# A four layer graph network on one core: side steps beside the differences get a half tile of their own

## The chip, the core and the metric

The kernel runs on one core of a Trainium2 chip. The core has five engines with instruction queues of their own: TensorE (PE in the profile; PEld is its loading of weights), VectorE (DVE), ScalarE (ACT), GpSimd (POOL) and SyncE (SP), which here issues the DMAs. Each engine takes its instructions in order, and one that waits holds up all behind it on that engine. The metric is the time of one execution on the device in microseconds; lower is better.

## The reference

There are 128 graphs of 128 nodes with 64 features, and a 128 x 128 adjacency matrix each, about an eighth of whose entries are not zero. Four layers follow each other. Each normalizes x over the features, clips it at zero, and adds what a small graph network makes of the result:

```python
# layer 0, h = relu(layernorm(x)); mask = adj > 0
xj_proj = x @ W1a
diff = x[:, :, None, :] - x[:, None, :, :]
h = jax.nn.relu(xj_proj[:, :, None, :] + diff @ W1b + b1)
hm = jnp.einsum('bjkh,bjk->bjh', h, mask)
return hm @ W2 + deg[..., None] * b2
# layer 1: three times relu(adj @ (h @ W + b)), then (h @ Wout + bout) * nodemask
# layer 2: y = (adj @ x + x) @ W + bias, normalized by its length, batch norm over all nodes, relu
# layer 3: tanh([h, adj @ h] @ W1 + b1) @ W2 + b2
```

Layer 0 needs a clipped sum for every edge, with 192 hidden features (x in these formulas is the layer's h). Layer 2's batch norm needs the mean over all graphs, so layers 2's end and 3 can only follow when every graph has been through layer 2's first part.

## The kernel before

Graphs are taken four at a time: 32 groups. For a group, layer 0 is done as 20 tiles (`ORDER`). The term that belongs to a node j (`psort`) is copied to PSUM, then a product of a selector with one bit per row (`oh`, made by comparing rank numbers on VectorE) and the node features `q` adds the term of that node's i-th neighbour, and VectorE clips the sum at zero and adds it to `acc`. One tile does this for one neighbour rank i of all nodes of the four graphs. To be exact in bf16, `q` is split in three parts. Twelve of the 20 tiles are "near": the first four ranks, with the three parts laid out over partitions by way of DRAM (`q_dram`, `near_q`, `n_dram`, `near_n`), so that each tile needs four products; the other eight are "far" and need twelve, or are made for the fullest rows alone (`psort_r`, `num_r`).

`differences(t)` issues one tile: products of the first two graphs, a fill of the tile after the next (L560), the selector of the tile three ahead (L541 for near ones, L546 for others), a `yield`, products of the last two, and the accumulation (L579 for a group's first tile, L581 on ScalarE for the first of the fullest rows, L583 else) and a second `yield`. So a tile has two halves, and a group 40. Three pairs of PSUM banks hold tiles (`blk`); two banks are left for all else.

Two other lines of work go beside the differences of a group g, as generators that are run a step at a time, up to their next `yield`:

- `prepare(g + 1)`: loads, the transposed adjacency (`adjT`, by TensorE and L391), the mask `mT`, the ranks of the neighbours and the order of the nodes (`rank`, `lower`, `to`), layer 0's norm, `q` and its split (L465 to L468), its way through DRAM (L469, L471), `num` and its way through DRAM (L483, L485), `fro` and `psort` with their copies (L498, L521).
- `after_layer0(g - 1)`: `layer0_end` (the sums `sA` and `sB` put back in node order, times W2), `layer1`, and `layer2_norm`. It takes nearly two groups of time, so two of these run beside each other, half a length apart.

When to take the next step is decided while the program is issued. Each generator has a count of halves since its start, a number of steps (`N_PREPARE` 14, `N_AFTER` 26) and a length in groups (0.8 and 1.9), and the generator that is furthest behind its share is stepped next. It is stepped at once when 2.5 steps late (`LAG`), else only while an estimate of TensorE's time (`spend`, called by every `matmul` and `transpose`) is below a budget that grows by `PACE` a half. A `yield 2` counts two steps. So a step has no place of its own: it depends on both counts and on the products issued until then, and several steps may fall in one half.

The order in which a program issues instructions is not wholly that in which they stand on the engines: in the trace, instructions that were ready stand ahead of others that were issued before them. Issue order decides between what is ready.

After the last group, the rest of the last two `after_layer0` run without differences beside them; then come the batch norm and layer 3.

## Time and profile before

| | |
|---|---|
| median of 3 runs | 1395.79 us (1392.44 to 1399.84) |
| the profiled execution | 1398.05 us |
| its span, first to last instruction | 1396.2 us |
| instructions | 29319 |
| busy: TensorE, VectorE, ScalarE, GpSimd | 1232.2, 1167.8, 990.8, 270.6 us |
| mean granted TensorE clock | 0.979 |
| first accumulation of a group (L579): first, last | 51.75, 1201.77 us |

The span has a start of some 50 us (weights, group 0's preparation), the 32 groups, a stretch to about 1270 us with the last graphs' layers 1 and 2, and the batch norm with layer 3. In a row of the groups view stand the line, the engine, what is written from what, the count, the busy time and the mean of one; in a row of waits: who waited, for whom, the total in us, how often, and the longest. A row of the timeline has the start in us, the duration, the engine and what it did, and in brackets the idle time before it. A row of the windows view has a stretch, its length, and the busy time of each engine with its count of instructions in brackets, then the granted clock, the share of DMA and its rate.

### The profile page before, as it was taken

The page shows a single profiled execution, that of the slowest core. Times are in us where ns is not written, and L with a number is a line of the kernel's source. Part 1 is how long each engine was busy: PE and PEld are TensorE (multiplying, and loading weights), DVE is VectorE, ACT ScalarE, POOL GpSimd, SP SyncE. Part 2 cuts the span into 40 slices and gives each one's busy share as a digit, 9 for nine tenths or more (in the row PEclk, how much of TensorE's full clock was granted, in tenths as well). Part 3 has the DMA queues.
Part 4 walks back from the last instruction along what each step waited for, and adds up shares of the span by engine and source line. Part 5 has one row for each costly group of instructions (what it writes and reads, how often), then busy time and mean ns, then how long its engine had stood idle before and what let it go on. Part 6 is the DMA issues. An engine that isn't in the chain of part 4 may idle for free.

```text
span 1396.2 us, 29319 instructions
## 1 busy us (share of the span) xinstructions
PE 1232.2 (88%) x10964; PEld 959.3 (69%) x10964; DVE 1167.8 (84%) x2629; ACT 990.8 (71%) x1883; POOL 270.6 (19%) x322
## 2 busy tenths in 40 slices
PE   3788999999999999999999999999999999995787
PEld 1467777777777777777777777776777777763566
DVE  6898888888888888888888888888898888866973
ACT  1677777777777777777777777777777777753783
POOL 3111111111111111111111111111111111015830
PEclk9899999999999999999999999999999999997889
DMA  5443222322323222222222222223222212200345
GB/s 120 131 120 98 67 66 78 83 83 84 83 76 83 84 75 75 76 63 75 66 78 84 83 84 83 75 83 84 76 75 79 62 59 60 76 9 15 93 112 126
DMA packets 108788, 110.97 MB, mean 79 GB/s; under 512 B 42895, under 2 KB 88220, under 8 KB 108636
## 3 DMA queue, kind: packets, MB, share of 16 engines
q1 hardware_dynamic: 108636, 109.00, 28.5%
q8 instruction: 89, 1.46, 0.5%
q14 instruction: 63, 0.52, 0.1%
HBM read 52.70 MB, written 35.29 MB: 63 GB/s over the span
## 4 chain that ended last, share of the span: by engine, by line
PE 65%; ACT 17%; DVE 13%; issue 2%; SPq 1%; DMA 1%; DVEq 0%; POOL 0%; ACTq 0%; POOLq 0%
PE blk L103 24%; PE ps_pr L103 10%; ACT blk L560 9%; DVE acc L583 6%; PE ps_ag L103 5%; PE ps_p L103 5%; PE ps_sA L103 5%; PE ps_o L103 3%; PE ps_sB L103 3%; PE ps_q L103 2%; PE ps_ah L103 2%; PE ps_hm L103 2%; ACT q L465 2%; DVE leftT L424 1%; PE ps_key L103 1%
## 5 line engine op out<-in xcount | busy, mean ns | idle before, releaser
L583 DVE SCALAR_TENSOR_TENSOR acc<-blk,acc 128x768 f32<-128x768 f32 x576 | 543.1, 950 | 65.0 <-PE blk L103 38.9
L560 ACT COPY blk<-psort 128x768 f32<-128x768 f32 x544 | 436.1, 806 | 134.1 <-DVE acc L583 132.2
L103 PE MATMUL blk<-q,oh 128*128 128x192 bf16 x3072 | 318.2, 246 | 34.5 <-ACT blk L560 34.3
L103 PEld LDWEIGHTS <-oh 128*128 128x128 bf16 x3072 | 259.1, 98 | 89.3 <-issue 84.3
L103 PE MATMUL blk<-near_q,ohn 128*128 128x192 bf16 x1536 | 199.7, 246 | 22.4 <-ACT blk L560 22.1
L103 PEld LDWEIGHTS <-ohn 128*128 128x128 bf16 x1536 | 134.7, 98 | 59.9 <-issue 45.3
L468 POOL TENSOR_TENSOR q<-rest,q 128x768 bf16<-128x768 f32 x32 | 52.8, 1648 | 209.1 <-ACT q L467 209.1
L642 POOL TENSOR_TENSOR adjT<-adjT,ident 128x512 f32<-128x512 f32 x32 | 41.9, 1310 | 254.8 <-PE ps_ag L103 254.8
L668 POOL TENSOR_TENSOR y<-y,nrm 128x256 f32<-128x256 f32 x32 | 19.7, 615 | 363.7 <-PE blk L103 238.1
L634 ACT COPY msg<-ps_pr 128x512 f32<-128x512 f32 x64 | 37.5, 586 | 68.9 <-PE ps_pr L103 67.5
L541 DVE TENSOR_SCALAR ohn<-near_n 128x1536 bf16<-128x1536 bf16 x128 | 84.3, 695 | 0.0
L103 PE MATMUL ps_pr<-g,dT 128*128 128x128 f32 x512 | 78.8, 288 | 0.8 <-ACT dT L626 0.8
L560 ACT COPY blk<-psort_r 128x768 f32<-128x768 f32 x96 | 77.5, 807 | 0.5 <-DVE acc L583 0.4
L103 PEld LDWEIGHTS ps_pr<-g,dT 128*128 128x128 f32 x512 | 64.3, 191 | 11.5 <-issue 7.2
L103 PE MATMUL ps_ag<-adjT,msg 128*128 128x128 f32 x512 | 71.5, 283 | 0.6 <-ACT msg L634 0.5
L103 PEld LDWEIGHTS <-ones_b 3*128 3x128 bf16 (+2 forms) x280 | 26.0, 93 | 59.1 <-issue 51.5
L103 PEld LDWEIGHTS ps_ag<-adjT,msg 128*128 128x128 f32 x512 | 62.1, 191 | 5.9 <-ACT msg L634 5.5
L103 PE MATMUL ps_p<-wp,hs 128*128 128x384 f32 x128 | 59.0, 543 | 0.0
L626 ACT ACTIVATE dT<-ps_ag 128x512 f32<-128x512 f32 x96 | 56.8, 592 | 3.0 <-PE ps_ag L103 2.8
L103 PE MATMUL ps_q<-wq,hT 128*128 128x384 f32 x128 | 52.5, 534 | 4.4 <-ACT hT L328 0.8
L103 PE MATMUL ps_hm<-ident,h 128*64 128x128 f32 x248 | 43.6, 308 | 14.0 <-ACT h L841 13.9
L103 PE MATMUL ps_sA<-fro,acc 128*128 128x128 f32 x256 | 53.3, 290 | 2.1 <-ACT dT L626 1.9
(220 smaller groups left out, 2544.8 us busy)
## 6 DMA issues: line engine op xcount, KB each, us to landing
q_dram<-q SPq DMA_DIRECT2D x32, 567.0 KB
near_q<-q_dram SPq DMA_DIRECT2D x96, 189.0 KB
near_n<-n_dram SPq DMA_DIRECT2D x96, 126.0 KB
a<-in_adj_dram SPq DMA_DIRECT2D x32, 256.0 KB
adjT_dram<-adjT SPq DMA_DIRECT2D x32, 256.0 KB
adjT<-adjT_dram SPq DMA_DIRECT2D x32, 256.0 KB
psort_r<-psort SPq DMA_DIRECT2D x32, 228.0 KB
fro_r<-fro SPq DMA_DIRECT2D x32, 152.0 KB
```

The costliest lines, as they stand in the source:

```text
L103: return nc.tensor.matmul(o, w, x, **kw)
L424: nc.vector.scalar_tensor_tensor(flat(leftT), pk, float(NEAR), flat(mT), ALU.is_gt, ALU.mult)
L465: nc.scalar.copy(parts_q[:, 0, p, :], pq[:, 0:W])
L468: nc.gpsimd.tensor_tensor(parts_q[:, 2], rest, parts_q[:, 1], ALU.subtract)
L541: nc.vector.tensor_scalar(oh.rearrange("p t b n -> p (t b n)"), near_n[g % 2].rearrange("p t b n -> p (t b n)"), float(i + 1), None, ALU.i ...
L560: nc.scalar.copy(columns(t), psorts[g][in_segments(n)])
L583: nc.vector.scalar_tensor_tensor(acc, o, 0.0, acc, ALU.max, ALU.add)
L626: nc.scalar.activation(flat(dT), pa, AF.Relu)
L634: nc.scalar.copy(flat(msg), pm)
L642: nc.gpsimd.tensor_tensor(adjT, adjT, ident.unsqueeze(1).to_broadcast([P, G, P]), ALU.add)
L668: nc.gpsimd.tensor_tensor(y, y, over_f(nrm), ALU.mult)
```

## The change

Each step now says itself how many halves pass until the next: `yield 3` means three. A generator holds the half at which its next step is due and the half it has reached. At each half, both generators take the steps that are due, whatever the others did. The numbers in the yields come from a search that evens the summed load of the three engines over a group's 40 halves. `prepare` then ends at its half 32, and `after_layer0` at its half 79, so that it takes two whole groups. The estimate of TensorE's time, the budget and their constants go.

Some work moves between steps as well: in `center` the square (L301) is issued with the mean and the centred x instead of a step later; `sA` and `sB` are no longer in adjacent steps, and `sB`'s bank is asked for at its own step; `prepare` takes the rest of its norm at fixed places, and issues `num` with its DMAs in the step that issues the split of `q`, ahead of `hs`, `db` and x's sum on GpSimd.

```diff
-    def matmul(o, w, x, **kw):
-        spend(w, math.prod(x.shape[1:]), x.dtype)
-        return nc.tensor.matmul(o, w, x, **kw)
...
+    matmul, transpose = nc.tensor.matmul, nc.tensor.transpose
...
         nc.vector.scalar_tensor_tensor(xc, over_f(mean), -1.0 / F, xt, ALU.mult, ALU.add)
-        yield
         sq = (once if tag else work).tile([P, G, F], F32, tag="sq" + tag, name="sq")
         nc.scalar.activation(sq, xc, AF.Square)
-        yield
+        yield 3
...
+    def finish(gen):
+
+        while True:
+            try:
+                next(gen)
+            except StopIteration as end:
+                return end.value
...
         mT = once.tile([P, G, P], BF16, tag="mT", name="mT")
-        yield
-        nc.vector.tensor_scalar(mT, adjT, 0.0, None, ALU.is_gt)
         ln = layernorm_relu(xt, "0")
         next(ln)
-        yield
+        yield 4
+        next(ln)
+        nc.vector.tensor_scalar(mT, adjT, 0.0, None, ALU.is_gt)
+        yield 2
         pr = bank("ps_rank")
...
-        yield
+        yield 4
         pr = bank("ps_rank")
...
-        next(ln)
         lower = once.tile([P, G, P], BF16, tag="lower", name="lower")
...
-        yield
+        yield 5
+        h = finish(ln)
+        yield 1
         pl = bank("ps_place")
...
-        next(ln)
-        yield 2
-        h = yield from ln
+        yield 1
         hT = transposed(h, "0")
-        yield
+        yield 3
         rest = once.tile([P, NP, W], F32, tag="rest", name="rest")
         for p in range(NP):
             pq = bank("ps_q")
             matmul(pq[:, 0:W], hT[:, p, :], flat(wq), start=True, stop=True)
-            yield
             nc.scalar.copy(parts_q[:, 0, p, :], pq[:, 0:W])
             nc.vector.tensor_tensor(rest[:, p, :], pq[:, 0:W], parts_q[:, 0, p, :], ALU.subtract)
+            yield 1 + p
         nc.scalar.copy(parts_q[:, 1], rest)
...
-        hs = gathered(h, to, "hs")
-
-        db = once.tile([P, G, F], F32, tag="db", name="db")
-        nc.gpsimd.tensor_tensor(db, over_f(degs[:, :, 0]), over_g(b2_all), ALU.mult)
-        nc.gpsimd.tensor_tensor(xt, xt, db, ALU.add)
-        yield
         pn = bank("ps_num")
...
-        yield
+        yield 2
+        hs = gathered(h, to, "hs")
+
+        db = once.tile([P, G, F], F32, tag="db", name="db")
+        nc.gpsimd.tensor_tensor(db, over_f(degs[:, :, 0]), over_g(b2_all), ALU.mult)
+        nc.gpsimd.tensor_tensor(xt, xt, db, ALU.add)
+        yield 1
         half, at = divmod(g, NG // 2)
...
-        yield
+        yield 3
         psort = edge.tile([P, NP, W], F32, tag="psort", name="psort")
...
             nc.scalar.copy(psort[:, p, :], pp[:, 0:W])
-            yield
+            if p == 0:
+                yield 3
...
     def layer0_end(g):
         xt, (_, _, fro, fro_r) = xs[g], sorts[g]
-
-        pA, pB = bank("ps_sA"), bank("ps_sB")
+        yield 4
+
+        pA = bank("ps_sA")
...
-            if b % 2:
-                yield
+            if b == 1:
+                yield 1
         nc.scalar.copy(flat(sA), pA)
+        yield 10
+        pB = bank("ps_sB")
...
         nc.scalar.copy(flat(sB), pB[:, 0 : NP * P])
-        yield 2
+        yield 9
...
-        for nxt, nrow, width in ((g1, "L1_gnn_b1", P), (g2, "L1_gnn_b2", P), (gout, "L1_gnn_bout", F)):
+        for nxt, nrow, width, wait in ((g1, "L1_gnn_b1", P, 3), (g2, "L1_gnn_b2", P, 3), (gout, "L1_gnn_bout", F, 4)):
...
-            yield
+            yield wait
...
-            yield
+            yield 7 if nxt is g1 else 3
...
-                    budget += PACE
-                    for s in side:
-                        s[3] += 1
-                    while side:
-                        late, s = max(((s[2] * s[3] / (nyields * s[4]) - s[1], s) for s in side), key=lambda k: k[0])
-                        if late <= 0 or (spent["us"] >= budget and late < LAG):
-                            break
-                        step = next(s[0], "end")
-                        s[1] += 1 if step is None else step if step != "end" else 0
-                        if step == "end":
-                            side.remove(s)
-                    budget = min(budget, spent["us"] + PACE)
+                    for s in list(side):
+                        while s in side and s[1] <= s[2]:
+                            step = next(s[0], None)
+                            if step is None:
+                                side.remove(s)
+                            else:
+                                s[1] += step
+                        s[2] += 1
```

In the norm (`layernorm_relu`) the two later steps follow after 3 and 3 halves, and `h` after 2; the other yields behind layer 0 become 3 (its end), 3 (`ah`), 4 (layer 1's end), 3 (`zT`), 3 (`py`), 2 (`nrm`) and 1 (`counted`).

## The prediction

> **What bounds the kernel now.** I read the page's busy times and slices first, to see whether one engine bounds the span.
>
> ```profile
> PE 1232.2 (88%) x10964; PEld 959.3 (69%) x10964; DVE 1167.8 (84%) x2629; ACT 990.8 (71%) x1883; POOL 270.6 (19%) x322
> PE   3788999999999999999999999999999999995787
> DVE  6898888888888888888888888888898888866973
> ACT  1677777777777777777777777777777777753783
> ```
>
> The kernel is one long steady stretch (slices 4 to 34) in which TensorE and VectorE are both nearly full and neither is full. Ends of products are modelled, so TensorE's nines overstate it. The steady stretch repeats by group, and a group starts with the one line L579. Its starts 600.00, 637.89, 675.68, 712.76 give 112.76/3 = 37.6 us a group. Next, the busy time of each engine in one group, cut where tiles 0, 5, 10 and 15 are accumulated:
>
> ```profile
> core 0: us, PE busy (x) PEld busy (x) DVE busy (x) ACT busy (x) POOL busy (x), PEclk, DMA share, GB/s
> 600.00:609.55 9.55, 8.95 (x95) 7.56 (x95) 8.48 (x17) 5.96 (x10) 2.61 (x3) 1.00 0.19 60
> 609.55:619.67 10.12, 8.30 (x75) 6.66 (x75) 9.06 (x21) 6.62 (x13) 1.34 (x2) 1.00 0.00 0
> 619.67:626.43 6.76, 6.32 (x59) 4.60 (x56) 6.73 (x19) 6.34 (x13) 1.65 (x1) 1.00 0.42 133
> 626.43:637.89 11.46, 11.45 (x90) 8.49 (x89) 8.52 (x20) 9.59 (x20) 0.61 (x1) 1.00 0.57 127
> ```
>
> Five tiles take 6.76 us in one place and 11.46 in another. VectorE is the fuller in the second and third rows (9.06 of 10.12, 6.73 of 6.76), TensorE in the first and last (11.45 of 11.46). That is what uneven placement looks like: each engine has its own crowded part and is short of work elsewhere. The waits say the same, over 32 groups:
>
> ```profile
> ACT blk L560 <- DVE acc L583: 132.6, 153, 2.4
> PE blk L103 <- ACT blk L560: 60.1, 107, 1.6
> DVE acc L583 <- PE blk L103: 38.9, 65, 1.6
> DVE mT L413 <- ACT adjT L391: 33.2, 29, 1.9
> PEld ps_sB L103 <- DVE leftT L424: 23.8, 29, 0.8
> ```
>
> The first three are the loop of the differences itself (fill, product, accumulate), each engine waiting for another in turn. The last two are side steps issued too close to what they need. Last, the end of a group, from the timeline:
>
> ```profile
> 619.70 1.65 POOL L468 TENSOR_TENSOR q<-rest,q 128x768 bf16<-128x768 f32 x1 [6.45 <-ACT q L467]
> 621.38 0.34 SPq L469 DMA_DIRECT2D q_dram<-q  x1
> 627.94 1.23 SPq L485 DMA_DIRECT2D near_n<-n_dram  x3
> 634.26 0.60 PE L108 MATMUL ps_aT<-ident,a 128*128 128x128 f32 x4
> 635.28 1.02 DVE L541 TENSOR_SCALAR ohn<-near_n 128x1536 bf16<-128x1536 bf16 x2
> 637.36 0.49 PE L103 MATMUL blk<-near_q,ohn 128*128 128x192 bf16 x4
> 637.89 0.96 DVE L579 SCALAR_TENSOR_TENSOR acc<-blk,extra 128x768 f32<-128x768 f32 x1 [0.89 <-PE blk L103]
> ```
>
> Here the reader sees a second chain: the split of q goes through POOL, SP and DRAM, and only its return lets the next group's tile 0 be made. The next group's transposes (634.26) already stand ahead of that tile on TensorE, although they are issued after it. So issue order is a preference: what is ready can be put ahead.
>
> **The change, part by part.** No instruction is added or dropped, so the engines' busy sums stay. The removed TensorE estimate issued nothing. What changes is where in the 40 half tiles of a group each side step is issued. I price a step by starts apart in the timeline where the engine does not idle (an accumulation 0.87 though its row says 0.95, a fill 0.73, a far half tile's six passes 0.50, a near one's two 0.17, an f32 pass 0.11). The positions before come from following the two counters and the budget through one group; those after are the sums of the yields.
>
> ```
> step (TensorE, VectorE, ScalarE us)   half before -> after
> prepare: transpose .44/0/.47          0 -> 0
>   first norm part 0/.66/.32           4, 10 -> 0
>   its var 0/.33/.20; h 0/.43/0        14; 14 -> 4; 15
>   mT 0/.34/0                          4 -> 4
>   rank1 .44/1.27/0                    8 -> 6
>   rank2 .65/2.10/0                    10 -> 10
>   place .11/.60/0; hT .22/0/.27       14; 16 -> 16; 17
>   q products .66/.46/.37 twice        17, 18, 20 -> 20, 21
>   last q cast 0/0/.81; num .22/0/.57  20; 22 -> 23; 23
>   hs .44/0/.27; fro .32/.58/.48       20; 25 -> 25; 26
>   psort .91/0/.37 twice; extra 0/0/1.38   27, 30; 32 -> 29, 32; 32
> after layer 0: sA .90 twice; copy .48 0, 4; 8 -> 4, 5; 5
>   sB .87/0/.33; po 1.34/.33/0         8; 14 -> 15; 24
>   ah, first ag and dT                 29; 32 -> 35; 38
>   (second group) pm, ag, pm, ag, gout 35, 38, 1, 5, 11 -> 1, 8, 11, 14, 18
>   zT, py, nrm, counted, sums          24, 27, 31, 34, 36 -> 30, 33, 36, 38, 39
>   two norms: xc, sq, var, h           14, 16, 18, 20 -> 27, 27, 30, 33
>                                       17, 18, 20, 23 -> 22, 22, 25, 28
> ```
>
> Example, VectorE in halves 8 to 11. Before: two accumulations 1.74, rank1 1.27, rank2 2.10, the product with the mask L640 0.34, one selector 0.20: 5.65 us. After: rank1 and L640 are elsewhere, 4.04. Doing this for each four halves, and taking the fullest engine of each:
>
> ```
> halves  0-3  4-7  8-11 12-15 16-19 20-23 24-27 28-31 32-35 36-39  sum
> before 3.83 3.41 5.65  4.55  3.39  3.69  3.82  2.47  3.82  2.67  37.3
> after  2.93 4.34 4.04  3.10  2.88  3.91  3.44  2.69  4.23  2.63  34.2
> ```
>
> The sum before, 37.3, is close to the measured 37.6, so I take this grain. It gives 3.1 us a group as the upper bound of the gain.
>
> Waits that go: sB (half 15) no longer shares its half with rank1 and rank2, whose banks it waited for in 29 groups (23.8 us); mT gets four halves after the transpose instead of a bad place in VectorE's queue (33.2 us). What is late next is ScalarE in halves 20 to 27 and 32 to 35 (3.91 and 4.23 us are its loads), where fills stand behind casts and extra. These terms are inside the table and not added.
>
> One rule of the Trainium skill speaks against this. Perfetto Trace Analysis, in Optimization Strategy, says that the same gap repeating can mean too few buffers for the next tile; the side steps have two banks, and the wait for leftT repeats in 29 groups. By that rule order alone would leave this wait, and the forecast would be 24 us later; the new positions put the bank users in different halves, so I follow the row.
>
> The lower bound comes from the q chain. The last q cast moves from half 20 to 23, and num from 22 to 23, while the halves get shorter. After the cast come POOL's L468, then on SP q_dram, n_dram, three near_q and three near_n; behind those wait fro_r and psort_r, which have the rest of the group. Waiting for near_n on VectorE is L541; behind it would stand the accumulation of tile 0, mT and the next norm. From tile 0 to the cast the table after gives 21.2 (halves 0 to 23) less 2.0 for the first two: 19.2 us; before it was 618.80 - 600.00 = 18.8. From the cast to q_dram 621.38 - 618.80 = 2.6. From q_dram to the next L579 the trace has 14.5 at the shortest (96.92 to 111.38) and 16.5 in the group shown (621.38 to 637.89). So a group bound by this chain takes 19.2 + 2.6 + 14.5 = 36.3, a gain of 1.3, or with 16.5 takes 38.3, a loss of 0.7.
>
> I take 35.3 us, a gain of 2.3: halfway between the evened load with the 0.3 by which the table missed (34.5) and the chain at its shortest (36.3), since the transposes at 634.26 show that a late tile 0 lets the next preparation run ahead and so shortens the chain. Group 1 has half of the old layer work, 1.2; groups 2 to 30 have 29 times 2.3 = 66.7; group 0 (25.50 us, preparation alone, VectorE 24.41 busy) and group 31 and the tail after 1231 keep their time: the same number of steps of the last two groups remains, about 13, and it costs 1 us either way if not.
>
> Moved past other queues at no cost: POOL's adjT L642 (1.3 us) now ends near half 20, before L468; hs needs POOL's cast of to, nine halves earlier; adjT's last reader zT is at half 30 instead of 24, ten halves before its buffer of four is written again. If one of these covers went, its cost would be its own length, at most 1.6 us a group.
>
> Sum against the profiled execution: 1398.05 (span 1396.2 and 1.85 around it) less 67.9 is 1330.1. That execution was 2.3 above the median 1395.79, so 1328.
>
> **The rivals.** First, full evening: group 34.5, 3.1 times 29.5 = 91 us, 1304. For it: 34.5 still leaves VectorE at 32.8 busy. Against: the three engines wait for each other in turn already.
>
> Second, the other side: the q chain becomes the bound. Place: L541 at the group's end. It decides when last cast to next L579 exceeds 37.6 - 19.2 = 18.4 us; the group shown has 19.1. At 38.3 a group it costs 0.7 times 29, 20 us: 1416; if halves stay 0.94 us, 23 of them less one and 19.1 make 39.8 and 1460. For it: L541 stands after tile 19's accumulation now. Against: VectorE's idle time before L541 is nil, so near_n lands earlier than it is used.
>
> Third, the order does little, since ready work is put ahead anyway: 1396. For it: group 0 took 25.50 where the same table gives 30.1. Against: the full groups do agree with the table.
>
> **How the numbers follow.** Likeliest case (35.3) 0.42, full evening 0.22, chain bound 0.26, little change 0.10. A change of 0.5% is about what the runs of this kernel can tell. Faster: 0.42 + 0.22 + 0.04 of the third = 0.68; same 0.06; slower 0.26. The range goes from 1288 (full evening and half a microsecond a group more) to 1412, just short of the chain's first price; alone, the likeliest case has 1310 to 1358 (gains of 2.9 to 1.3).
>
> **What would show it.** Right: L579 about 35.3 us apart; five tiles taking between 8 and 9.5 us everywhere; sB's wait for leftT and mT's for adjT gone; fills waiting for accumulations under 132.6. Wrong: VectorE idle before L541 or before L579 growing past the 0.89 shown, near_n issued within 3 us of the next L579, or ScalarE full in the third quarter with TensorE waiting for fills beyond 60.1.

## The result: 0.55% slower, and the profile after

The changed kernel takes 1406.09 us (median, 1397.23 to 1408.77), the kernel before beside it on the same chip 1398.46. The ratio is 1.0055, with a 95% interval of 1.0044 to 1.0066. The forecast was 1328 us.

The busy times and slices of the changed kernel:

```profile
PE 1230.3 (88%) x10964; PEld 964.5 (69%) x10964; DVE 1150.2 (82%) x2629; ACT 995.6 (71%) x1883; POOL 278.6 (20%) x322
PE   3788999899989989999999999998999999895787
DVE  6798788889889889888878888988988888866873
```

The same work is done, and VectorE's share is lower than before (82%, it was 84%). Its busy time is 17.6 us less, and 17.3 of that lie in the near selectors, first before, then after (busy time, mean ns of one; idle time ahead of them):

```profile
L541 DVE TENSOR_SCALAR ohn<-near_n 128x1536 bf16<-128x1536 bf16 x128 | 84.3, 695 | 0.0
L529 DVE TENSOR_SCALAR ohn<-near_n 128x1536 bf16<-128x1536 bf16 x128 | 67.0, 559 | 0.0
```

The median of one is the same (553 and 552 ns). But before, one selector in each of 28 groups took 1.15 us (the one at 620.62, for instance, beside GpSimd's q, 619.70 to 621.35), and after, none takes over 0.97; that GpSimd's work is the cause was not tried. The forecast did not count on this, and the time does not show it: VectorE waits longer instead.

By the starts of groups (now L567), the profiled execution's span, 8.3 us longer than before, divides into 5.4 up to the start of group 3 (153.54, was 148.13), 0.9 for the 28 groups from there to group 31, and 2.0 behind that. So the groups, of which 2.3 us each had been forecast, gained nothing: they take 0.03 us more each.

Three groups in a row, in the windows view (length, then busy time and number of instructions by engine, the granted clock, DMA):

```profile
core 0: us, PE busy (x) PEld busy (x) DVE busy (x) ACT busy (x) POOL busy (x), PEclk, DMA share, GB/s
563.76:603.10 39.34, 36.01 (x330) 29.10 (x330) 32.88 (x73) 29.08 (x55) 6.56 (x7) 1.00 0.28 78
603.10:641.67 38.57, 34.74 (x316) 27.67 (x315) 32.70 (x71) 28.17 (x53) 6.41 (x7) 1.00 0.28 76
641.67:676.15 34.48, 31.96 (x288) 24.76 (x287) 31.41 (x68) 27.82 (x52) 6.39 (x7) 1.00 0.28 79
```

Groups now come in a cycle of three lengths, 34.5 to 39.3 us (before: 37.1 to 37.9). The last row looks like full evening come true (34.5 was the first rival's group), but its instruction counts say otherwise: 288 products instead of 330. Side work of that group was done in the next one. The mean of the three, 37.5, is what counts.

The waits of the whole span (who waited, for whom, total in us, times, longest):

```profile
ACT blk L548 <- DVE acc L571: 51.2, 113, 1.0
DVE to_b L441 <- PE ps_place L439: 44.7, 30, 1.9
...
PE blk L556 <- ACT blk L548: 37.8, 68, 2.2
DVE acc L571 <- PE blk L556: 36.2, 68, 2.2
...
DVE mT L404 <- ACT adjT L379: 14.8, 20, 1.2
```

Fills waiting for accumulations fell from 132.6 to 51.2 (those that wait for a group's first accumulation rose from 1.7 to 23.7), TensorE's waits for fills from 60.1 to 37.8, mT's from 33.2 to 14.8, and sB's wait for leftT is no longer among them (layer 1's aggregation has some of it now, 8.8 us in 11 groups). But a wait stands on VectorE that the kernel before does not have: `to_b`, the comparison with the sort positions, waits 1.5 us in 30 of 32 groups. The timeline of the second group above shows why:

```profile
613.46 1.16 PE L629 MATMUL ps_ag<-adjT,msg 128*128 128x128 f32 x8 [0.73 <-ACT msg L625]
613.67 0.96 DVE L571 SCALAR_TENSOR_TENSOR acc<-blk,acc 128x768 f32<-128x768 f32 x1
...
614.54 0.45 PE L592 MATMUL ps_sB<-fro,acc 128*64 128x128 f32 x4
...
615.25 0.44 PE L592 MATMUL ps_sB<-fro_r,acc 128*64 128x128 f32 x4
...
615.62 0.67 PE L556 MATMUL blk<-q,oh 128*128 128x192 bf16 x6
...
616.12 0.24 PE L439 MATMUL ps_place<-ones_b,lower 128*128 128x1 bf16 x4
...
616.23 0.66 PE L556 MATMUL blk<-q,oh 128*128 128x192 bf16 x6
616.41 0.69 DVE L441 TENSOR_TENSOR to_b<-row_b,ps_place 128x512 bf16<-128x512 bf16 x1 [1.78 <-PE ps_place L439]
...
617.01 0.95 DVE L571 SCALAR_TENSOR_TENSOR acc<-blk,acc 128x768 f32<-128x768 f32 x1
```

Read TensorE's rows alone: aggregation, then the eight products of sB (half 15 of the table), six products of a tile, and only then the four tiny ones that give the positions (half 16). VectorE is free from 614.63, but the next thing in its queue is `to_b`, and no accumulation can pass it. From 613.67 to 617.01 one accumulation is started in 3.34 us. Neither engine is overloaded in these halves by the prediction's table; one stands behind the other's queue. It does so twice: the accumulation at 617.01 also needs its tile's second six products (616.23, to 616.89), and they too stand behind sB. So these rows don't tell whether the late positions or the late products are the price of sB's place.

### The profile page after: what moved, and what is told of

Its sections match the earlier page's. It is cut to its first block, busy times and chain, and to the rows that moved or that the text cites. A ratio compares the mean times of both kernels' runs of the same rounds, so it can differ in the third digit from the quotient of the medians.

```text
span 1404.5 us, 29255 instructions
## 1 busy us (share of the span) xinstructions
PE 1230.3 (88%) x10964; PEld 964.5 (69%) x10964; DVE 1150.2 (82%) x2629; ACT 995.6 (71%) x1883; POOL 278.6 (20%) x322
## 4 chain that ended last, share of the span: by engine, by line
PE 63%; ACT 16%; DVE 15%; issue 3%; SPq 1%; DMA 1%; POOL 0%; ACTq 0%; DVEq 0%; POOLq 0%
PE blk L556 19%; PE ps_pr L621 7%; DVE acc L571 7%; ACT blk L548 5%; PE ps_ag L629 5%; PE ps_sA L584 3%; PE ps_ga L326 3%; PE ps_p L503 3%; PE ps_sB L592 2%; PE ps_pr L334 2%; PE blk L664 2%; PE ps_hm L829 2%; DVE rest L452 2%; PE ps_o L600 2%; PE ps_o L598 2%
## 5 line engine op out<-in xcount | busy, mean ns | idle before, releaser
L571 DVE SCALAR_TENSOR_TENSOR acc<-blk,acc 128x768 f32<-128x768 f32 x576 | 546.0, 951 | 41.0 <-PE blk L556 36.2
L548 ACT COPY blk<-psort 128x768 f32<-128x768 f32 x544 | 434.6, 807 | 67.4 <-DVE acc L571 38.5
L556 PE MATMUL blk<-q,oh 128*128 128x192 bf16 x3072 | 323.2, 247 | 35.4 <-ACT blk L548 35.2
L617 ACT ACTIVATE dT<-ps_ag 128x512 f32<-128x512 f32 x96 | 57.1, 595 | 41.7 <-PE ps_ag L629 40.6
L471 POOL TENSOR_TENSOR db<-degs,b_all 128x256 f32<-128x256 bf16 x32 | 19.6, 613 | 253.3 <-DVE degs L417 253.3
L529 DVE TENSOR_SCALAR ohn<-near_n 128x1536 bf16<-128x1536 bf16 x128 | 67.0, 559 | 0.0
L441 DVE TENSOR_TENSOR to_b<-row_b,ps_place 128x512 bf16<-128x512 bf16 x32 | 22.0, 686 | 44.7 <-PE ps_place L439 44.7
L450 PE MATMUL ps_q<-wq,hT 128*128 128x384 f32 x128 | 56.1, 525 | 0.8 <-ACT hT L316 0.8
```

Of the source, the lines that this page charges most:

```text
L450: matmul(pq[:, 0:W], hT[:, p, :], flat(wq), start=True, stop=True)
L529: nc.vector.tensor_scalar(oh.rearrange("p t b n -> p (t b n)"), near_n[g % 2].rearrange("p t b n -> p (t b n)"), float(i + 1), None, ALU.i ...
L548: nc.scalar.copy(columns(t), psorts[g][in_segments(n)])
L556: matmul(of(o, b), oh[:, b, :], of(q, b), start=False, stop=True, skip_group_check=True)
L571: nc.vector.scalar_tensor_tensor(acc, o, 0.0, acc, ALU.max, ALU.add)
L617: nc.scalar.activation(flat(dT), pa, AF.Relu)
```

## The experiments

Times are medians, ratios are to the kernel before on the same chip (1397 to 1399 us in all batches), with 95% intervals. "Steady stretch" is 150 to 1180 us of the span, where nothing else is said. "Table" is the sum of the fullest engine over four halves by the prediction's prices (37.3 before, 34.2 after); for the other kernels it was worked out in the same way, and the working isn't shown.

### First: the near tiles, the places, the shared banks

**Two far tiles first in each five.** This gives q, which only near tiles wait for, more time, in the changed kernel and in the kernel before.

```diff
-ORDER = [(NEARS, OTHERS)[k] for k in (0, 1, 0, 1, 0)] * 4
+ORDER = [(NEARS, OTHERS)[k] for k in (1, 1, 0, 0, 0)] * 4
```

> The changed kernel with the order of the 20 tiles of a group turned so that two far tiles come first (pattern far, far, near, near, near instead of near, far, near, far, near); nothing else. A far tile needs nothing that has been through DRAM, so the return of q and num may come two tiles later. Theory of the q chain (the group's end waits for near_n's way through DRAM): the gap between the last accumulation of a group and the first of the next, now 4.8, 6.3 and 3.5 us in three kinds of group, falls to some 2 us in all of them, a group goes from 37.5 to about 35 us, the whole from 1406 to about 1330. Theory of the shared banks (side sums that lie in the banks of the tile buffers tie steps to tiles, so that groups differ by the buffer that tile 0 takes): three kinds of group remain, 1395 to 1406. If the loop of fills, products and accumulations is itself the limit: no change within 10 us.

Measured: 1376.29 us, 0.9862 (0.9824 to 0.9900), faster than both kernels.

> The same turn of the order of tiles in the kernel before. Theory of the q chain: the gap at a group's end there, 4.0 to 4.6 us, falls to some 2 us, a group from 37.6 to 35.5, the whole from 1398 to about 1335; the two kernels then differ by what their placement is worth, the changed one some 10 us or more ahead. Theory of the shared banks: no change in the kernel before, whose groups hardly differ (37.1 to 37.9).

Measured: 1420.84 us, 1.0184 (1.0124 to 1.0244), slower. So it is not that near tiles come too early in general. In the changed kernel VectorE's wait for the positions fell with the order of the tiles, from 40.6 to 4.4 us in the steady stretch; that was the first hint at it.

**Only the preparation put back to the halves it had before.**

```
yield behind     mT rank1 rank2  h  to  hT  num  hs  fro
changed kernel    2   4     5    1   1   3   2    1   3
this run          4   2     4    0   2   1   0    5   2
```

> The changed kernel with fixed places, but the steps of the preparation put where the kernel before has them: rank1 at half 8, rank2 10, the rest of the norm and place 14, hT 16, q products 17 and 18, last cast, num and hs 20, fro 25, psort 27 and 30; the older group's steps stay at their new places. Theory of the q chain: the cast three halves earlier brings tile 0 of the next group forward by up to 2.8 us, so groups of 35 to 36 us and about 1350. Theory of the shared banks: three kinds of group, 1400 to 1410. If the evening of loads is what counts, it gets slower, as VectorE's crowd at half 14 is back: 1410 to 1440.

Measured: 1392.94 us, 0.9966 (0.9954 to 0.9978). The wait for the positions is 27.7 us there.

**The two sums that share a tile's banks given banks of their own.** `degs`' product and `ysum` lie in the banks of the differences' tiles, which go round in three; the edit takes them to the two side banks.

```diff
-        pd = degs_at[:, half, at * 2 * G : (at + 1) * 2 * G]
+        pd = bank("ps_pd")[:, 0 : 2 * G]
...
-        add_sums(ysum, counted, y)
+        pb = bank("ps_ys")
+        for p in range(NP):
+            matmul(pb[0:G, p * P : (p + 1) * P], counted, y[:, 2 * p : 2 * p + 2, :].rearrange("p b f -> p (b f)"), start=True, stop=True)
+        nc.vector.tensor_tensor(flat(ysum), flat(ysum), pb[0:G, 0 : NP * P], ALU.add)
```

> The changed kernel with the two side sums taken out of the banks of the tile buffers: the sorted degrees go to a side bank of their own, and the sums for the batch norm's mean to a side bank per group, added up in SBUF by one more small VectorE instruction a group (about 0.2 us). Theory of the shared banks: the groups of 39.3 and 38.6 us become like the one of 34.5, so all near 35 us and the whole near 1320. Theory of the q chain: the gaps at the end of a group stay at 3.5 to 6.3 us, and the whole moves by less than 15 us.

Measured: 1437.22 us, 1.0281 (1.0256 to 1.0307). The cycle of three lengths is gone (38.2 us a group, 39.7 where the clock fell), so the shared banks have to do with the cycle. Banks of their own do not make the kernel faster; but the edit also asks twice more for the two side banks and adds a VectorE instruction a group, so it does not price the sharing by itself.

### Second: the way through DRAM, and the places one by one

**q and num read in SBUF.** The near tiles read `q` and `num` where they are made; the DMAs are issued as before, and nobody reads what they bring. The near tiles' values are then not the reference's. The same two lines in both kernels:

```diff
-  nc.vector.tensor_scalar(oh.rearrange("p t b n -> p (t b n)"), near_n[g % 2].rearrange("p t b n -> p (t b n)"), float(i + 1), None, ALU.is_equal)
+  nc.vector.tensor_scalar(oh, sorts[g][0].unsqueeze(1).to_broadcast([P, 3, G, P]), float(i + 1), None, ALU.is_equal)
...
-  q = (proj if third is None else near_q)[g % 2][:, part]
+  q = proj[g % 2][:, part]
```

> The changed kernel with the near tiles made from what lies in SBUF already: the selectors compare num itself (shown three times by a broadcast), and the products read a part of q in place of near_q. All DMAs through DRAM are still issued and land, but nothing reads them; products, fills, accumulations and their sizes are the same, the values of the near tiles are not the reference's. Theory of the q chain: this is the whole price of the way through DRAM; tile 0 of the next group needs only num (half 23) and stands where it was issued, the gap at a group's end falls from 3.5 to 6.3 to about 2 us, and the whole goes from 1406 to about 1330. If the end of a group is only where lateness shows that has its cause elsewhere: 1370 to 1400, with the gap turning up in other tiles, as with the far tiles first (1376).

Measured: 1402.01 us, 1.0037 (1.0020 to 1.0055).

> The same in the kernel before. Theory of the q chain: also some 50 us or more faster than 1398, and the distance between this and the changed kernel without the way through DRAM is what the new places are worth by themselves (2.3 us a group, 67 us, by the forecast). If the way through DRAM costs nothing here: 1390 to 1400.

Measured: 1390.68 us, 0.9944 (0.9926 to 0.9962). The edit is not free: reading `num` by a broadcast, a near selector takes 944 ns (median) in the changed kernel and 943 in the one before, where it took 552 and 553, and VectorE's busy time grows by 45.4 and 20.9 us. So the gains of 0.2 and 0.6% are what is left after that, and do not price the return from DRAM. In the changed kernel the gain lies in the start: the first accumulation comes at 44.84 instead of 55.84 us, while a group from group 3 to group 31 takes 37.6 us, as it did. That the chain does not bound the groups there is read from the trace of the changed kernel: in the group from 603.10 the last near_n is issued by 631.18 us, the selectors that read it start at 640.27, and VectorE has no wait ahead of them in any group.

**The older group's steps put back to the halves they had, alone and with the preparation's.** These are the halves at which the counters and the budget of before had taken them.

```
yield            start  sA  sA copied  sB  po  h  msg1  msg2  dT3  x  zT  py  nrm  counted
changed kernel     4     1     10       9   3  2    7     3    4   4   3   3   2     1
this run           0     4      4       6   0  9    3     4    6   6   2   4   3     2
```

(`h` here is layer 1's norm; `msg1`, `msg2` and `dT3` are the messages and the last clipped product of layer 1; `x` is its end.)

> The changed kernel with only the older group's steps at the places of the kernel before, the preparation at its new ones. With the preparation at its old places the changed kernel took 1392.9. If the evening of the older group's steps is what gains and the later preparation what loses: slower than 1406, about 1415 to 1440. If neither matters: 1395 to 1410.

Measured: 1431.56 us, 1.0242 (1.0225 to 1.0259).

> The changed kernel's mechanism (fixed places, the same grouping of work into steps) with the places that the kernel before gives its steps, for the preparation and for the older group: sA 0 and 4, sB 8, po 14, first norm 14, 17, 20, ah 29, ag 32, pm 35, ag 38, pm 41, ag 45, gout 51, second norm 57, 60, 63, zT 65, py 67, nrm 71, counted 74, sums 76. It separates the places from the regrouping. If the places count: about the time of the kernel before, 1395 to 1402, and the even places are worth nothing against the crowded ones. If the regrouping (the square with the mean, num with the last cast, sB's bank at its own step) costs and the places gain: slower than the changed kernel, 1420 to 1470.

Measured: 1524.69 us, 1.0908 (1.0889 to 1.0926). This is the widest swing of all, with the same instructions as in the 1406 us kernel and with halves that the kernel before passed in 1398 us. So places matter greatly, against the third rival, and halves alone do not say what they cost. Which of the joined steps is so dear at these halves was not settled.

### Third: the pacing, and a wait that did not move

**The kernel before without its budget.** One condition goes; grouping and nominal places stay.

```diff
-                        if late <= 0 or (spent["us"] >= budget and late < LAG):
+                        if late <= 0:
```

> The kernel before with one condition taken out of its placing loop: a step beside the differences is issued as soon as it is due by its share of the halves, and is no longer held back while the estimated TensorE time is over 0.85 us per half tile. Grouping of the steps and their nominal places stay those of before. It prices the pacing alone. The theory that the pacing is what made before good, and that its loss is what after's even table only makes up for, expects most of the difference between before (1398 us) and the changed kernel with all its places put back (1525 us): 1470 us or more, and waits of PE for ACT's fills well over before's 45 us in the steady stretch. The theory that the regrouped steps (the num step joined to the last cast, the square to the mean, each with longer runs of TensorE and VectorE work behind one another) are what costs expects 1390 to 1420.

Measured: 1381.96 us, 0.9881 (0.9854 to 0.9909). Neither theory had this: the pacing, which the change drops too, cost the kernel before 1.2%. So the change contained a gain, and the rest of it lost 1.7%. The table has 38.5 for this kernel and 37.3 for the one with pacing.

**The changed kernel with both earlier gains.** Far tiles first, and the preparation put back.

```diff
-ORDER = [(NEARS, OTHERS)[k] for k in (0, 1, 0, 1, 0)] * 4
+ORDER = [(NEARS, OTHERS)[k] for k in (1, 1, 0, 0, 0)] * 4
# and prepare's yields as above
```

> The changed kernel with two edits that each were faster alone: two of the far tiles first in each five, so that the first near tiles come later (1376 us alone), and the preparation's steps at the halves they had before (1393 us alone, against 1406). If the two gains come from different waits (the boundary between two groups, and the wait of VectorE for the sort positions) they add up: 1360 to 1368. If both only move the preparation's late end away from the next group's first near tile, the second adds nothing: 1374 to 1384; and since the tables were made even for the other order, a loss of some 10 us (1385 to 1395) is possible too.

Measured: 1400.44 us, 1.0011 (0.9998 to 1.0024). Two gains of 30 and 13 us together make one of 6, although the wait for the positions is down to 11.9 us. Each alone had lowered that wait; together they have others (x's end on GpSimd, 22.7 us, and the rest of the q split, 15.8). So a low wait for the positions is not enough.

**The four products for the positions issued half a tile earlier.**

```diff
+        pl = bank("ps_place")
+        for b in range(G):
+            matmul(pl[:, b : b + 1], lower[:, b, :], ones_b[:, 0:1], start=True, stop=True)
         h = finish(ln)
         yield 1
-        pl = bank("ps_place")
-        for b in range(G):
-            matmul(pl[:, b : b + 1], lower[:, b, :], ones_b[:, 0:1], start=True, stop=True)
```

> The changed kernel with the four small matmuls that give the sort positions issued one half tile earlier, ahead of the step that ends the first normalization; VectorE's comparison with them stays in its half. The wait of VectorE for these matmuls (40.6 us in 27 waits in the steady stretch, the longest kind of wait on VectorE) should go. The theory that waits at the head of VectorE's queue took the gain expects that most of the 40.6 us comes back: 1365 to 1385. The theory that such a wait only stands for another one, because VectorE's next accumulation waits for TensorE anyway, expects 1398 to 1408, with the waits of the accumulations for TensorE grown by about as much.

Measured: 1407.44 us, 1.0060 (1.0037 to 1.0084). VectorE's waits in the steady stretch of this run:

```profile
DVE acc L571 <- PE blk L556: 35.2, 67, 2.2
DVE to_b L441 <- PE ps_place L437: 34.6, 25, 1.8
```

The wait was to go and did not (40.6 in the changed kernel). Issue order is a preference, and the products of sB still stood ahead. The run says little on what the wait costs.

**Before's budget on the new places.**

```diff
+PACE, LAG = 0.85, 7
...
-                    for s in list(side):
-                        while s in side and s[1] <= s[2]:
+                    budget += PACE
...
+                        late, s = max(((s[2] - s[1], s) for s in side), key=lambda k: k[0])
+                        if late <= 0 or (spent["us"] >= budget and late < LAG):
+                            break
...
+                    budget = min(budget, spent["us"] + PACE)
```

> The changed kernel's grouping and places, but with before's pacing on top: a step is held back while the estimated TensorE time is over 0.85 us per half, up to 7 halves behind its place. If before's pacing is what keeps TensorE's and ScalarE's fills in step, and the fixed places lack it, this is faster than the changed kernel: 1375 to 1395. If the even places are better left alone, since a step that comes later puts the even load out of balance and the next group's first tile later, it is slower: 1415 to 1440.

Measured: 1408.62 us, 1.0061 (1.0042 to 1.0080), with the group lengths of the changed kernel to 0.03 us wherever the clock was full, and the same order of instructions on VectorE up to the last graphs. So at these places the budget holds no step, and neither theory was tried.

### Fourth: grouping against places

**The changed grouping of the preparation alone, and the joined square alone, in the kernel before without its budget.**

```diff
# before_nb_prep: prepare in the changed grouping, old nominal places
-        yield
-        nc.vector.tensor_scalar(mT, adjT, 0.0, None, ALU.is_gt)
         ln = layernorm_relu(xt, "0")
         next(ln)
+        next(ln)
+        yield
+        next(ln)
+        nc.vector.tensor_scalar(mT, adjT, 0.0, None, ALU.is_gt)
         yield
...
+        h = finish(ln)
+        yield 0
...
# num and its DMAs behind the last cast, then hs, db, x
```

> The kernel before without its pacing (1382 us), with the preparation's steps grouped as in the changed kernel (the first normalization beginning with the transposed adjacency, its end ahead of the sort positions, projection and cast in one step, the ranks' step joined to the last cast and the gather behind it), each at its old nominal place. The theory that the regrouping of the preparation costs expects 1395 to 1430. The theory that the places cost, or the other regrouping, expects 1376 to 1388.

Measured: 1392.83 us, 0.9952 (0.9935 to 0.9969).

```diff
# before_nb_square: center
         nc.vector.scalar_tensor_tensor(xc, over_f(mean), -1.0 / F, xt, ALU.mult, ALU.add)
-        yield
...
         nc.scalar.activation(sq, xc, AF.Square)
-        yield
+        yield 2
# and one next(ln) less in prepare
```

> The kernel before without its pacing (1382 us), with the square issued in the same step as the mean and the centering, and nothing else. ScalarE then stands at the square until VectorE has centered, with fills queued behind it: three squares a group, and the centering takes two VectorE instructions of about 0.33 us each. The theory that this joint costs expects up to 0.7 us for each of the three: 2 us a group, 1400 to 1440 us. The theory that the work around it hides it expects 1376 to 1388.

Measured: 1380.74 us, 0.9874 (0.9852 to 0.9897). The joined square costs nothing here.

**The even places with the old grouping of the preparation and the square apart.**

```diff
# prepare as before, but at the halves of the change:
# yields 4, 2, 4, 6, 1, 3, 1, 2, 0, 3, 3, 3, 0
# center
+        yield 1
         sq = (once if tag else work).tile([P, G, F], F32, tag="sq" + tag, name="sq")
         nc.scalar.activation(sq, xc, AF.Square)
-        yield 3
+        yield 2
```

> The changed kernel with before's grouping of the preparation's steps and with the square in a step of its own again, one half behind the centering; every step at the half that the changed kernel gives it (the two accumulator sums apart as in the changed kernel, since they can't share a half at these places). The theory that the joined steps are what costs expects the even places to show their gain now: 1340 to 1380. The theory that the even places themselves cost more than they bring expects 1395 to 1420, as the changed kernel.

Measured: 1394.55 us, 0.9975 (0.9959 to 0.9992).

The last runs make a square, all without a budget:

| ratio to the kernel before | old places | even places |
|---|---|---|
| old grouping of the preparation | 0.9881 | 0.9975 |
| new grouping | 0.9952 | 1.0055 |

The lower right kernel, the changed one, has the joined square as well. Across, the even places cost 0.9 and 1.0%; down, the new grouping costs 0.7 and 0.8%; each difference is uncertain by 0.2 to 0.3 (intervals in quadrature). Minus 1.2 for the pacing, plus 0.9 and 0.8, is the 0.55% that was measured. The even places cost time although the table has them at 35.5 with the old grouping (38.5 without them).

**Far tiles first in the kernel before without its budget.** Both edits as shown.

> The kernel before without its pacing, with two far tiles first in each five. The far tiles first took 30 us off the changed kernel and added 22 us to the kernel before, where TensorE's clock was seen at 0.50 in eleven spells that the kernel before does not have (18.7 us of full clock in all). If the loss there came from the pacing's pile-ups of work ahead of the far tiles, this is 1350 to 1375; if the far tiles first only suit the changed kernel's late preparation, it is 1385 to 1410.

Measured: 1428.18 us, 1.0215 (1.0187 to 1.0244). Far tiles first are bad for the old places with and without pacing.

### Last: one step moved, against the table

The products of sB go from half 15 to half 19, out of the way of the positions. The sum of the yields stays, so nothing else of the older group moves.

```diff
         nc.scalar.copy(flat(sA), pA)
-        yield 10
+        yield 14
         pB = bank("ps_sB")
...
         nc.scalar.copy(flat(sB), pB[:, 0 : NP * P])
-        yield 9
+        yield 5
```

> The changed kernel with the sums sB (eight products and a copy) four halves later, at half 19 instead of 15, so that they no longer stand on TensorE between VectorE's lower and the sort positions. By the table of loads the sum of the fullest engine rises from 34.2 to 34.5 us a group: the theory that the table decides expects 1406 plus 0.3 times 29, 1410 to 1420. The theory that the wait of VectorE for the sort positions costs expects that wait to fall from 40.6 us in the steady stretch to below 15, and 1375 to 1395. If the wait falls and the time stays at 1400 to 1409, the waits only stand for one another.

Measured: 1355.99 us, 0.9701 (0.9684 to 0.9719): 50 us less than the changed kernel, 3.0% faster than the kernel before, and against the table's sign. Waits of VectorE in its whole span:

```profile
DVE t L631 <- PE ps_pr L621: 30.6, 30, 6.3
...
DVE acc L567 <- PE blk L556: 17.7, 23, 2.2
DVE x L601 <- PE ps_o L600: 14.3, 31, 0.6
DVE to_b L441 <- PE ps_place L439: 13.8, 29, 0.7
DVE mT L404 <- ACT adjT L379: 11.2, 26, 0.7
DVE acc L571 <- PE blk L556: 9.9, 34, 0.7
```

The wait for the positions is 13.8 us instead of 44.7, and that of the other accumulations for TensorE 9.9 instead of 36.2. The latter fits a knock-on that no run tries alone: an accumulation that is late frees its bank late, the fill is late, and the product after it. The same place of the timeline, the positions with TensorE's rows ahead of them:

```profile
593.91 1.16 PE L629 MATMUL ps_ag<-adjT,msg 128*128 128x128 f32 x8 [0.73 <-ACT msg L625]
...
594.42 0.96 DVE L571 SCALAR_TENSOR_TENSOR acc<-blk,acc 128x768 f32<-128x768 f32 x1
...
594.90 0.66 PE L556 MATMUL blk<-q,oh 128*128 128x192 bf16 x6
...
595.40 0.24 PE L439 MATMUL ps_place<-ones_b,lower 128*128 128x1 bf16 x4
...
595.68 0.69 DVE L441 TENSOR_TENSOR to_b<-row_b,ps_place 128x512 bf16<-128x512 bf16 x1 [0.29 <-PE ps_place L439]
...
596.28 0.95 DVE L571 SCALAR_TENSOR_TENSOR acc<-blk,acc 128x768 f32<-128x768 f32 x1
```

sB is gone from between, and VectorE waits 0.29 us instead of 1.78. The two accumulations around `to_b` start 1.86 us apart instead of 3.34; over 28 groups it is 2.05 us on average, and 3.09 in the changed kernel. Three groups of this run:

```profile
547.78:583.26 35.48, 33.86 (x309) 27.04 (x307) 32.10 (x69) 27.88 (x53) 6.22 (x7) 1.00 0.30 82
583.26:619.04 35.78, 33.79 (x307) 26.86 (x305) 32.35 (x71) 28.05 (x54) 6.23 (x7) 1.00 0.29 79
619.04:655.81 36.77, 34.74 (x320) 28.00 (x318) 33.35 (x72) 28.80 (x55) 6.57 (x7) 1.00 0.30 82
```

Groups take 36.0 us, 1.5 less than the three shown of the changed kernel, with the same busy time (mean TensorE 34.13 here, 34.24 there).

> The even places with the old grouping of the preparation (1394.5 us), with sB at half 19 in the same way. The wait for the sort positions there is 51.7 us, the longest of VectorE's. The theory that this wait is what the even places cost expects 1355 to 1380, below the kernel before without pacing (1382). The theory that the table decides expects 1398 to 1410; that the waits stand for one another, 1388 to 1398.

Measured: 1361.34 us, 0.9735 (0.9715 to 0.9755). The same edit takes 33 us off the even places with the old grouping, and the wait for the positions falls from 51.7 to 9.2 us (the latter over 150 to 1150 us, as its span is shorter). Wait and time do not go one for one: here 42 us of wait and 33 of time, in the changed kernel 31 and 50. With sB out of the way, the even places beat the old ones (0.9735 against 0.9881), as the forecast had it, and the new grouping no longer costs (0.9701 against 0.9735).

## Why the prediction was wrong

**Right.** No instruction that works on data came or went (the counts by engine are equal; there are 64 waits for semaphores fewer). The waits that it said would go went or shrank: sB's for leftT, mT's for adjT, fills' for accumulations. The Trainium skill's page Perfetto Trace Analysis, in Optimization Strategy, says that such a repeated gap can mean too few buffers; here sB's wait went with the two side banks as they are, as the prediction had it. Part of it came back at layer 1's aggregation (8.8 us), and in the run with the old grouping at the even places all of it (23.2 us in 29 groups); in the best run 1.0 us is left. The queue order remark, that issue order is a preference, was right too, and the earlier issue of the four products showed it again.

**The step that failed: "These terms are inside the table and not added".** The table treated four halves as a bin in which three engines work freely, and so it priced waits that go, and none that come. It had "place .11/.60" at half 16 and sB at half 15, both in uncrowded bins (3.10 and 2.88 us); it did not ask what stands on TensorE ahead of what VectorE needs next. That was sB, 1.08 us by its starts (614.54 to 615.62; priced at .87), directly behind an aggregation of the same length (613.46 to 614.54): 2.16 us of side work in one piece, in two of the four halves of a bin that had 3.10. The positions and a tile's products came behind it, and VectorE's queue stood still for 1.5 us in nearly every group. Moving sB alone took 50 us off, which is 42 against the kernel before, of the 68 that were forecast for the groups. Whether the positions or the tile's products carry the price was not separated.

**The grain itself was not supported.** That the table's sum before, 37.3, was close to the measured 37.6 was taken as proof. Over these runs it does not order the times:

```
                         table   group measured, us
before                   37.3    37.6
before, no budget        38.5    37.1
changed                  34.2    37.6
changed, far first       37.3    36.9
changed, both put back   37.6    41.8
changed, sB at 19        34.5    36.1
```

**"The removed TensorE estimate issued nothing"** was true and no reason to cost it at nothing: the pacing it drove cost 16 us. That gain is in the result, hidden under the loss.

**The regrouped preparation** was moved in the table and not priced as a regrouping; it cost 10 us, by the runs in the kernel before without budget.

**The likeliest case's 35.3 us** was taken half way between full evening (34.5) and the shortest chain (36.3), two figures of which neither was met. TensorE is busy for 34.2 us of a group in the windows above, and the prediction's prices have less for it: a far half tile is .50, and the rows above have 0.66 for the same six products. Taken from starts apart, the prices leave out the ends of bursts that the profile counts. Whichever is nearer the truth, the bound by the profile's busy time leaves 3.4 us of 37.6, and reaching it would need a TensorE that never waits. The best run, 36.1, is about 2 above.

**Start and tail** were costed at nothing; they cost 5.4 and 2.0 us in the profiled execution. Of the 5.4, 4.1 lie ahead of group 0's first accumulation (55.84, was 51.75), where the first preparation runs alone and its places can even nothing.

**The rivals.** The chain of q gave 1416 and is nearest in time on the slower side, but its mechanism was not seen: the list of VectorE's waits has none before L529, the near selector, and near_n was issued 9 us ahead of it in the group looked at. What the way through DRAM costs by itself stays open, since the run that reads q in SBUF (4 us faster) pays for dearer selectors. "Order does little" gave 1396 and fell: the same work was timed between 1356 and 1525 us. Full evening was not reached.

**The marks.** Accumulations L567 apart by 37.6 and not 35.3: wrong. Five tiles between 8 and 9.5 us: in the group from 603.10 they take 8.41, 9.11, 8.05 and 13.01; three quarters were evened, and the last, with the group's end, took it all back (there VectorE waits 1.19 us for adjT at mT and 0.90 for the norm's rstd, both ahead of the selectors of the next tile 0). Fills waiting below 132.6: right, and it did not help. TensorE waiting for fills beyond 60.1: it was 37.8, so that the trouble did not show where it was looked for.

**What stays open:** why the new grouping without the budget is 127 us slower than before at the halves that before's pacing reached, and costs only 10 at the nominal ones; what makes the remaining 2 us of a group in the best run; and which of the two hand-overs behind sB is the dear one. That run is also the version to keep.

## What to carry to other kernels

A table of loads per slot bounds a schedule from below and does not rank schedules: with queues that run in order, work whose result another engine needs next should not stand behind a large product that nobody is waiting for. So after evening loads, list each hand-over between engines, and ask what stands ahead of the producer and what is queued behind the consumer. Then look in the trace for the longest new wait and move what stands ahead of its producer, and time it, since a wait that goes can leave another behind; the Trainium skill's page Perfetto Trace Analysis says as much in Optimization Strategy (find what blocks the engine, and make that start sooner), and here it was worth 50 us where the search had lost 8.

## What was not expected of the hardware

TensorE's granted clock fell to half in spells of 3.4 or 6.8 us in the steady stretch, none in the kernel before, two in the changed one, nine where the sums had banks of their own, eleven with far tiles first in the kernel before. The windows of the changed kernel around one of them:

```profile
690.00:700.00 10.00, 9.79 (x99) 8.08 (x98) 8.22 (x18) 7.63 (x14) 3.29 (x4) 1.00 0.00 0
700.00:705.00 5.00, 3.38 (x28) 2.10 (x27) 4.93 (x17) 4.93 (x11) 0.00 (x0) 0.98 0.66 196
705.00:710.00 5.00, 5.00 (x20) 3.42 (x20) 1.81 (x5) 3.05 (x9) 0.00 (x0) 0.50 0.69 194
710.00:715.00 5.00, 4.78 (x36) 3.91 (x34) 3.50 (x9) 3.68 (x8) 0.00 (x0) 0.84 0.27 75
```

TensorE is idle for 1.62 us of the second row, in one piece; in the third its clock is 0.50. The group with this spell took 42.5 us where its like take 39.3. The same wait stands in nine groups, and in seven no spell follows; the run with the budget, in the same order, has four such spells at other groups. So what falls on whom is partly chance, and it may be what spreads this kernel's times (1397 to 1409). In the kernel before with far tiles first no TensorE idle time is over 1 us, and the clock falls all the same:

```profile
400.00:405.00 5.00, 3.55 (x31) 2.36 (x31) 4.07 (x15) 5.00 (x10) 1.64 (x1) 1.00 0.40 122
405.00:408.50 3.50, 3.50 (x16) 2.49 (x15) 2.91 (x10) 2.04 (x6) 0.00 (x0) 0.52 0.59 177
```

There TensorE had been busy for 3.55 of 5 us. The Trainium skill's page TensorE: Matmul & The Clock Gate, in Why this matters for your kernels, warns of idle gaps of more than about 3 us. By these rows shorter ones are enough at times, single ones of 1.62 us or several that add up to about 1.45 in 5. Waits that TensorE can take without harm to the sum of its work can thus have a second price, about 1.6 to 3.2 us each time (40.9 and 42.5 us groups against 39.3).
